# A four-stage graph network kernel: layer 0 gets a stage of its own, layers 1 and 2 share one

## The chip, the cores and the metric

The kernel runs on one core of one Trainium2 chip. The time is device microseconds of that core for the whole program, from start to end of one execution. The unchanged kernel was timed three times: 5719.75, 5727.59 and 5731.36 us, median 5727.59.

The engines are named as in the profile: PE multiplies matrices (PEld is its weight load), DVE works element by element and reduces, ACT computes activation functions and copies, SP issues DMA transfers. POOL does next to nothing here. PE's results land in PSUM, and DVE or ACT carry them on to SBUF.

## What is computed

The input is 64 independent graphs ("items") of 256 nodes with 128 features each, and a 0/1 adjacency matrix per item of 256 x 256 with about one entry in eight set. Four graph layers follow each other. After each one, the layer's input is added and the sum is normalised over the features.

```python
x = _layernorm(x + L0(x, adj))   # max over neighbours j of relu(p_i + q_j + b)
x = _layernorm(x + L1(x, adj))   # three ELU projections, adj @ in, adj.T @ out, tanh of an update
x = _layernorm(x + L2(x, adj))   # ELU twice, then two graph convolutions with D^-1/2 (A+I) D^-1/2
x = _layernorm(x + L3(x, adj))   # sum over neighbours j of gelu(layernorm(m_j + m_i + b)), update, layernorm
```

Layers 0 and 3 are the heavy ones: they compute one 128-feature message for each pair of node and neighbour, layer 0 reducing by maximum and layer 3 by a sum. Layers 1 and 2 are chains of small matrix products with ELU, tanh and layernorm between them.

## The kernel before

**Slots instead of a dense adjacency.** For each half h of the nodes j (128 of them) the kernel sorts the 256 nodes i by their number of neighbours in that half. With the nodes sorted, slot k holds the k-th neighbour of each node, and the slots' widths can shrink: 40 slots together are WIDTH columns, instead of 128 x 256. `hot` is a 0/1 matrix in fp8 that picks for each column its neighbour: PE multiplies the neighbours' features with it, in 512-column groups, in three bf16 parts each (three matmuls that add up). `lack` and `lack_t` mark columns that have no neighbour, and a few short matmuls (L681) push these out of the maximum.

**The parts of an item's work**, with the lines of the kernel before:

- *Sort and one-hots* (in `first`, L502 to L643): load `x0` and `an` (the adjacency); `nz` (L509) and its transpose `aT`; count neighbours (L528, L534); rank the nodes by ACT's Sign with an accumulator (L551); compare each rank `place` with a row of numbers to get the permutation matrices `perm` (L560); permute (L566), transpose them to `permT` (L577, L581); place the neighbours (L585), build `lack`; build `hot` with 24 comparisons and two more operations on DVE (L629, L635). The `fulls` flags go to memory by eight DMA issues (L620).
- *Layer 0* (in `first`, L644 to L712): a product of the transposed x with two weights (L647), three bf16 parts `q3`, then two times ten groups of three matmuls L665 with the `lack` matmuls, each group folded into `lanes` by DVE with a maximum (L492, called from `fold`), a maximum over the lanes `total_m` (L688), transposed (L691), back to the nodes' order (L699), the maximum of both halves `m` (L706), residual and layernorm: `x1`.
- *Layer 1* (`layer_1`, called by `second`): transpose (L207), L223, `io` (L226), ELU, L230 and `nd`, the two adjacency products L238 and L240 into `ag`, L249, `y` (L253), tanh, layernorm: `x2`.
- *Layer 2* (`layer_2`, called by `third`): L285, `hs` (L288), ELU twice, then twice: scale (L293), adjacency product L296, copy `agg` (L299), weight product L304, `hs` (L308); layernorm: `x3`.
- *Layer 3's first part* (in `third`): transpose, L797, copies `dn` and the three bf16 parts `c3` (L497 to L500), the product with `perm` L810, `dT`, and the first four of ten tiles of messages (`sums_of`): groups of three matmuls L728, added to `dT` into `pre` (L732), squared by ACT (`sq`, L736), summed over the features by PE (L743) and copied to `row` (L745); the row goes to memory, comes back in another shape, and becomes the scale 1/sqrt for each column (L74, L75), which goes to memory again.
- *Layer 3* (`last`): the scales come back, spread over the partitions (`rs_s`), `pre` is multiplied by them (L839), ACT takes Gelu (L841), DVE folds the tiles into `sums` (L492), and the remaining six tiles of `sums_of` run in between. The products L860, L870, L325, an update, two layernorms and the store end the item.

**Stages and steps.** All 64 items are unrolled. In one step, four stages work on four different items: `last` on one, `third` on the next, `second` and `first` on the two after it. Each stage is a Python generator that yields at points in its work, and `together` (L341) interleaves the stages in proportion to a number beside each of them in `STAGES` (L879), so that all four spread over the step. These numbers are `last` 34, `third` 34, `second` 14 and `first` 44. There are three steps in which the pipeline fills and three in which it drains.

**What sets the order.** The order in which the generators issue instructions is not the order on the engines: a scheduler places the instructions engine by engine, within what the buffers allow. Each engine then works through its own list strictly in order; an instruction at the head that waits holds up all behind it. PSUM has four tiles `mm` for short products and four tiles `bigp` for the 512-column groups, each kind used in turn. In the middle of the run the order repeats every two items.

ACT holds one table of functions at a time. Square, copies, Sign and Identity run with any of those used here; Gelu, Sqrt and Exp (and sometimes Tanh) each have an ACT_TABLE_LOAD in front where the function before was of another kind.

Of the kernel before, what the change touches and what calls it, by code (L numbers as in the profile page):

```python
# [9 lines left out]
F32 = mybir.dt.float32  # L10
# [33 lines left out]
def kernel(  # L44
# [17 lines left out]

    ident = consts.tile([P, P], F32, name="ident")
    make_identity(nc, ident)
    half = consts.tile([P, N], F32, name="half")
    nc.vector.memset(half, 0.5)
    eps_t = consts.tile([P, 1], F32, name="eps_t")
    nc.vector.memset(eps_t, EPS)
    minus1 = consts.tile([P, 1], F32, name="minus1")
# [284 lines left out]
    def sparse(ctx):  # L354
# [12 lines left out]
        nc.vector.tensor_copy(ident_b, ident)  # L367
        upto = cs.tile([P, P], BF16, name="upto")
        iota_k = cs.tile([P, N], F32, name="iota_k")
        down = cs.tile([1, N], BF16, name="down")  # L370
        slot1 = cs.tile([P, SLOTS], BF16, name="slot1")
        part1 = cs.tile([P, 1], F32, name="part1")
# [17 lines left out]
        with tc.tile_pool(name="cs_prep", bufs=1) as pp:  # L390
            t = pp.tile([P, P], F32, name="upto_f")
            nc.gpsimd.affine_select(
                out=t, in_=ones, compare_op=ALU.is_ge, fill=0.0, base=0, pattern=[[1, P]], channel_multiplier=-1
            )
            nc.vector.scalar_tensor_tensor(upto, ident, -FAR, t, ALU.mult, ALU.add)
            t = pp.tile([P, N], I32, name="iota_i")
            nc.gpsimd.iota(t, pattern=[[1, N]], base=0, channel_multiplier=0)
            nc.vector.tensor_copy(iota_k, t)
            t = pp.tile([P, 1], I32, name="part_i")
            nc.gpsimd.iota(t, pattern=[[0, 1]], base=0, channel_multiplier=1)  # L400
            part = pp.tile([P, 1], F32, name="part")
            nc.vector.tensor_copy(part, t)
            nc.vector.tensor_scalar(part1, part, 2.0, None, ALU.subtract)
            nc.vector.memset(part1[:3], float(SLOTS))
            nc.vector.tensor_scalar(down, iota_k[:1], -1.0, float(N - 1), ALU.mult, ALU.add)
            nc.vector.tensor_scalar(slot1, iota_k[:, :SLOTS], 1.0 - FAR, None, ALU.add)
            for h in range(H):
                for c in range(H):
                    nc.vector.tensor_scalar(
                        down_c[:, h, c:c + 1], part, -1.0, float(N - 1 - h * P), ALU.mult, ALU.add  # L410
                    )
            for t, slots in ((most, [w for s0, n, w in RECTS for _ in range(n)]), (least, SURE)):
                row = pp.tile([P, N], F32, name="slots")
                nc.vector.memset(row, 0.0)
                for w in slots:
                    if w:
                        nc.vector.tensor_scalar(row[:, :w], row[:, :w], 1.0, None, ALU.add)
                if t is most:
                    nc.vector.tensor_scalar(cover, row[:3], float(SLOTS), None, ALU.subtract)
                for hk in range(H):  # L420
                    pt = ps_mm.tile([P, 512], F32, name="mm")
                    nc.tensor.transpose(pt[:, :P], row[:, hk * P:(hk + 1) * P], ident)
                    for h in range(H):
                        nc.vector.tensor_copy(t[:, h, hk:hk + 1], pt[:, :1])
            t = pp.tile([P, 1], F32, name="gbe")
            nc.scalar.activation(t, be3, AF.Gelu)
            t3 = pp.tile([P, 3], F32, name="gbe3")
            nc.vector.tensor_copy(t3, t.broadcast_to([P, 3]))
            pt = ps_mm.tile([P, 512], F32, name="mm")
            nc.tensor.matmul(pt[:3, :P], t3, w3u[:, 1], start=True, stop=True)  # L430
            rest = pp.tile([3, P], F32, name="u_rest")
            nc.vector.tensor_copy(rest, pt[:3, :P])
            total = pp.tile([3, P], F32, name="u_total")
            nc.vector.memset(total, 0.0)
            for i in range(3):
# [12 lines left out]
            nc.vector.tensor_copy(tail, t)  # L448
            nc.vector.memset(tail[:1, g_n - 1], 1.0)
# [51 lines left out]

        def first(g, s):  # L502

            xn = sh.node_tile("x0")
            nc.sync.dma_start(xn, x[ds(g, 1)].rearrange("b (h p) d -> p (b h) d", p=P))
            an = state.tile([P, H, N], F32, name="an")
            nc.sync.dma_start(an, adj[ds(g, 1)].rearrange("b (h p) j -> p (b h) j", p=P))
            nz = pair.tile([P, H, N], BF16, name="nz")
            nc.vector.tensor_scalar(nz, an, 1.0, None, ALU.is_equal)  # L509
# [9 lines left out]
                nc.scalar.copy(aT[:, hj], pt[:, :N])  # L519
            nzT = as_bf16(aT)  # L520
            yield
            xT = sh.to_features(xn, "xT_0", 1)


            pd = psum()
# [28 lines left out]
            yield  # L554
            pos = work.tile([P, H, H], F32, name="place")
            nc.vector.tensor_scalar(pos, more, 0.5, 0.5 * (N - 1), ALU.mult, ALU.add)
            perm = state.tile([P, H, H, N], F32, name="perm", bufs=3)
            for h in range(H):
                for hi in range(H):
                    nc.vector.tensor_scalar(perm[:, h, hi], iota_k, pos[:, h, hi:hi + 1], None, ALU.is_equal)  # L560
            perm_b = as_bf16(perm)
            yield
            pz = psum()
            for h in range(H):
# [41 lines left out]
                fl[:, 5:9].rearrange("p (a b) -> p a b", a=H), fv, -1.0, least, ALU.mult, ALU.add  # L606
            )
            nc.vector.tensor_max(viol, viol, fl)
            lack_t = pair.tile([ROWS, H, g_n, g_w], BF16, name="lack_t")
            for h in range(H):  # L610
                nc.vector.tensor_mul(lack_t[:, h], tail, widen(lack[:, h, :g_w], g_n))
            s.update(an=an, aT=aT, perm=perm, permT=permT, lack=lack)

            full = pair.tile([ROWS, H, N], BF16, name="full")
            nc.vector.tensor_scalar(full, lack, 0.0, None, ALU.is_equal)
# [18 lines left out]
            for h in range(H):  # L634
# [4 lines left out]
                    ALU.is_equal,  # L639
                    saturate=False,  # L640
                )
            yield
            s["hot"] = hot  # L643

            pq = psum()
            for h in range(H):
                nc.tensor.matmul(  # L647
# [129 lines left out]

        def second(g, s):

            yield from sh.layer_1(s, s["an"], s["aT"], s["x1"])  # L780

        def third(g, s):

            dg = s["dg"]

            def deg_of(deg):
                nc.vector.tensor_scalar(deg, dg, 1.0 / N, None, ALU.mult)

            yield from sh.layer_2(s, s["aT"], deg_of)
            yield  # L790
            x3, perm = s["x3"], s["perm"]

            x3T = sh.to_features(x3, "x3T")
            yield
            pc = psum()
            for h in range(H):
                nc.tensor.matmul(  # L797
                    pc[:, h * N:(h + 1) * N], x3T[:, h * P:(h + 1) * P], w3c.rearrange("p c o -> p (c o)"),
                    start=True, stop=True,
                )  # L800
            pcv = pc.rearrange("p (h c o) -> p h c o", h=H, c=2)
            dn = work.tile([P, H, P], F32, name="dn")
            nc.scalar.copy(dn, pcv[:, :, 1])
            c3 = state.tile([P, 3, H, P], BF16, name="c3")
            split3(c3, pcv[:, :, 0])
            yield
            pd = psum()
            for h in range(H):
                for hi in range(H):
                    nc.tensor.matmul(  # L810
                        pd[:, h * N:(h + 1) * N], dn[:, hi], perm[:, h, hi], start=hi == 0, stop=hi == H - 1
                    )
            yield
            dT = state.tile([P, H, N], F32, name="dT")
            nc.scalar.activation(dT, pd.rearrange("p (h n) -> p h n", h=H), AF.Identity, bias=b3c)
            s.update(x3T=x3T, c3=c3, dT=dT)
            yield
            for i in range(AHEAD):
                yield from sums_of(s, i)
# [56 lines left out]


        U = next(u for u in (UNROLL, 8, 4, 2, 1) if B % u == 0)
        STAGES = [(last, 34), (third, 34), (second, 14), (first, 44)]  # L879

        def steps(g0):
            ss = [{} for _ in range(U)]
# [12 lines left out]
    def general(ctx):  # L895
# [10 lines left out]
        sh = Shared(work, state, ps_mm)  # L906
        psum = sh.psum
        ones3 = cs.tile([3, P], BF16, name="ones3")

        def split3(dst, src):  # L910

# [165 lines left out]

        def run():
            nc.vector.memset(ones3, 1.0)

            with tc.For_i(0, B, U) as g0:
                ss = [{} for _ in range(U)]
# [60 lines left out]
```

## Time and profile before

| | |
|---|---|
| median of three runs | 5727.59 us |
| the profiled execution | 5731.62 us |
| its span | 5729.7 us |
| busy PE / DVE / ACT | 4529.9 / 4834.4 / 4275.2 us |
| granted PE clock, mean over the run | 0.862 |
| HBM traffic over the span | 63 GB/s |
| first comparison of item 0 (`nz`) | at 35.6 us |
| first comparison of item 63 | at 5411.1 us |
| table loads on ACT | 1236, 1283 ns each |

How to read the profile: a group of the form "L560 DVE perm" is all instructions of line 560 that write the tile `perm`. Its busy time is the time in which at least one of them runs, so that busy time over count is what one adds when neighbours overlap. "PE mm L566 <- DVE perm L560: 245.5, 64, 5.1" means that PE, at L566, waited for DVE's L560 for 245.5 us in total, 64 times, the longest 5.1 us. The chain is followed back from the last instruction; each piece is what the next one waited for, or the instruction before it on the same engine. A stretch in the windows view gives for each engine the busy time within that stretch and the number of instructions.

### The profile page before, as it was taken

To read this page: it belongs to the slowest core of one execution; us is meant where nothing else is said; L and a number is where in the kernel's file an instruction comes from. 1 tells how busy PE (TensorE), PEld (TensorE's weight loads), DVE (VectorE), ACT (ScalarE), POOL (GpSimd) and SP (SyncE) were. 2 spreads that over 40 slices of the span, in tenths; PEclk is the share of its full clock that TensorE was granted. 3 is DMA by queue.
4 is the path that set the end of the run, shared out by engine and by line. 5 is a ranking of instruction groups with operands and counts; after the bars stand their busy time and mean duration, and the time that the engine had idled before them with its cause. 6 is when DMAs were issued, how large, how long until landed. Compare 5 with 4: busy or idle time off the path is not lost.

```text
span 5729.7 us, 83531 instructions
## 1 busy us (share of the span) xinstructions
PE 4529.9 (79%) x27408; PEld 2508.7 (44%) x27408; DVE 4834.4 (84%) x14654; ACT 4275.2 (75%) x6485; POOL 1.9 (0%) x10
## 2 busy tenths in 40 slices
PE   5878878878778778788788788787887887877875
PEld 2444444444444444444444444444444444444443
DVE  6788888888888888888888888888888888888876
ACT  2577777777777777777777777777777777777785
POOL 0000000000000000000000000000000000000000
PEclk8888889889889889888898898898888887888986
DMA  0122222222212221221221222122212212221222
GB/s 22 44 70 63 62 63 72 62 63 66 69 57 70 65 63 63 72 63 62 63 72 62 63 65 70 59 68 65 63 62 72 64 62 63 69 66 60 68 65 74
DMA packets 292813, 365.15 MB, mean 64 GB/s; under 512 B 151952, under 2 KB 210448, under 8 KB 292368
## 3 DMA queue, kind: packets, MB, share of 16 engines
q1 hardware_dynamic: 292368, 359.73, 20.0%
q8 instruction: 217, 3.56, 0.3%
q14 instruction: 228, 1.87, 0.1%
HBM read 345.07 MB, written 14.53 MB: 63 GB/s over the span
## 4 chain that ended last, share of the span: by engine, by line
PE 52%; DVE 29%; ACT 11%; issue 4%; DMA 3%; SPq 0%; DVEq 0%; POOL 0%; ACTq 0%
PE bigp L665 11%; PE bigp L728 8%; DVE pre L839 6%; PE mm L860 5%; DVE lanes L492 4%; PE mm L743 4%; DVE hot L629 4%; DVE pre L732 4%; DVE sums L492 3%; PE bigp L681 3%; DMA rs_s<-scale_line 2%; PE mm L870 2%; PE mm L296 2%; PE mm L699 2%; PE mm L647 2%
## 5 line engine op out<-in xcount | busy, mean ns | idle before, releaser
L665 PE MATMUL bigp<-hot,q 128*128 128x512 fp8e4 (+1 forms) x3840 | 1052.3, 371 | 66.6 <-DVE lanes L492 52.6
L728 PE MATMUL bigp<-hot,c 128*128 128x512 fp8e4 (+1 forms) x3840 | 928.8, 372 | 140.2 <-DVE pre L732 140.2
L732 DVE TENSOR_TENSOR pre<-bigp,dT 128x512 f32<-128x512 f32 (+6 forms) x1664 | 846.3, 530 | 37.8 <-PE bigp L728 33.5
L492 DVE TENSOR_TENSOR lanes<-bigp,lanes 128x512 f32<-128x512 f32 (+6 forms) x1536 | 772.7, 503 | 94.6 <-PE bigp L681 86.9
L839 DVE TENSOR_TENSOR pre<-pre,rs_s 128x1024 f32<-128x1024 f32 (+1 forms) x640 | 732.9, 1150 | 48.6 <-DMA rs_s<-scale_line 48.0
L736 ACT ACTIVATE sq<-pre 128x1024 f32<-128x1024 f32 (+1 forms) x640 | 638.5, 998 | 169.9 <-DVE pre L732 163.9
L841 ACT ACT_TABLE_LOAD x535 | 686.4, 1283 | 9.5
L492 DVE TENSOR_TENSOR sums<-pre,sums 128x1024 f32<-128x1024 f32 (+6 forms) x1024 | 628.8, 614 | 41.2 <-ACT pre L841 40.7
L745 ACT ACTIVATE row<-mm,eps_t 128x256 f32<-128x256 f32 (+1 forms) x640 | 289.6, 453 | 476.9 <-PE mm L743 476.7
L841 ACT ACTIVATE pre<-pre,be,g 128x1024 f32<-128x1024 f32 (+1 forms) x512 | 594.2, 1172 | 57.8 <-DVE pre L839 53.0
L743 PE MATMUL mm<-sq,ones 128*32 128x256 f32 (+1 forms) x5120 | 482.9, 440 | 135.2 <-ACT sq L736 135.2
L74 ACT ACT_TABLE_LOAD x445 | 570.9, 1283 | 7.5
L728 PEld LDWEIGHTS <-c 128*128 128x128 bf16 x3840 | 331.2, 98 | 550.5 <-issue 136.1
L665 PEld LDWEIGHTS <-q 128*128 128x128 bf16 x3840 | 310.8, 97 | 392.6 <-issue 112.0
L296 PE MATMUL mm<-aT,hs 128*128 128x256 f32 x512 | 232.3, 600 | 316.1 <-DVE hs L293 214.8
L629 DVE TENSOR_SCALAR hot<-rank 128x512 fp8e4<-128x512 bf16 (+5 forms) x1536 | 440.5, 348 | 0.0
L681 PEld LDWEIGHTS <-pick 42*128 42x128 bf16 x2944 | 155.8, 95 | 481.5 <-issue 474.2
L296 PEld LDWEIGHTS mm<-aT,hs 128*128 128x128 f32 x512 | 135.6, 293 | 425.8 <-issue 316.1
L860 PE MATMUL mm<-w3u,sums 128*128 128x128 f32 x2048 | 296.7, 289 | 18.4 <-DVE sums L492 16.1
L194 ACT ACT_TABLE_LOAD x221 | 283.5, 1283 | 3.9
L681 PE MATMUL bigp<-lack,pick 42*128 42x36 bf16 (+16 forms) x2944 | 285.7, 187 | 0.0
L860 PEld LDWEIGHTS mm<-w3u,sums 128*128 128x128 f32 x2048 | 254.5, 195 | 37.3 <-issue 17.6
(226 smaller groups left out, 7132.6 us busy)
## 6 DMA issues: line engine op xcount, KB each, us to landing
rs_s<-scale_line SPq DMA_DIRECT2D x512, 512.0 KB
rs_s<-scale_line SPq DMA_DIRECT2D x128, 352.0 KB
an<-in_adj SPq DMA_DIRECT2D x64, 256.0 KB
x<-in_x SPq DMA_DIRECT2D x64, 128.0 KB
line<-row SPq DMA_DIRECT2D x512, 4.0 KB
out<-o SPq DMA_DIRECT2D x64, 128.0 KB
fu<-fulls SPq DMA_DIRECT2D x192, 4.0 KB
vr<-line SPq DMA_DIRECT2D x192, 8.0 KB
```

Source lines behind the costliest of these rows:

```text
L74: nc.scalar.activation(t, t, AF.Sqrt)
L492: nc.vector.tensor_tensor(lanes[:, :k, :w], src[:, i:i + k], lanes[:, :k, :w], op)
L629: nc.vector.tensor_scalar(hot[:, :, at:at + w], rank[:, :, :w], s0 + i + 1.0 - FAR, None, ALU.is_equal, saturate=False)
L665: nc.tensor.matmul(pt[:, :tl], q3[:, i, h], hot[:, h, t0:t0 + tl], start=i == 0, stop=False)
L681: nc.tensor.matmul(o_, l_, r_, start=False, stop=i == len(todo) - 1)
L728: nc.tensor.matmul(pt[:, :bl], c3[:, k, h], hot[:, h, t0 + b:t0 + b + bl], start=k == 0, stop=k == 2)
L732: nc.vector.tensor_add(block(pre[:, b:], n, w, at), block(pt, n, w, at), widen(dT[:, h, :w], n))
L736: nc.scalar.activation(sq[:, :tl], pre[:, :tl], AF.Square)
L743: nc.tensor.matmul(pr[q * Q:(q + 1) * Q, :tl // 4], ones[:, :Q], v4[:, :, q], start=True, stop=True)
L839: nc.vector.tensor_mul(pre[:, :tl], pre[:, :tl], rs[:, :tl])
L841: nc.scalar.activation(msg[:, :tl], pre[:, :tl], AF.Gelu, bias=be3, scale=g3)
L860: nc.tensor.matmul(pt[:, cols], lanes[:, k, cols], w3u[:, 1], start=k == 0, stop=False)
```

## The change

Layer 0 moves out of `first` into a function `layer_0`, which `second` now runs; layer 1 moves from `second` to `third`, ahead of layer 2. So the four stages are: sort and one-hots; layer 0; layers 1 and 2 with layer 3's first four tiles; layer 3. The numbers in `STAGES` become 34, 48, 28 and 17.

Tiles that now live for more steps get more buffers or another pool: `x0` and `an` have three, and `lack_t` moves to the pool `state`, where it has two. `perm` becomes bf16, written by comparing a bf16 row of numbers; layer 3, which multiplies with it in f32, makes an f32 copy `perm_f` on ACT for each item. The tile `half` is made only in the general path, which does not run with these inputs.

```diff
-            xn = sh.node_tile("x0")
+            xn = state.tile([P, H, P], F32, name="x0", bufs=3)
...
-            an = state.tile([P, H, N], F32, name="an")
+            an = state.tile([P, H, N], F32, name="an", bufs=3)
...
-            xT = sh.to_features(xn, "xT_0", 1)
...
-            perm = state.tile([P, H, H, N], F32, name="perm", bufs=3)
+            perm = state.tile([P, H, H, N], BF16, name="perm", bufs=3)
             for h in range(H):
                 for hi in range(H):
-                    nc.vector.tensor_scalar(perm[:, h, hi], iota_k, pos[:, h, hi:hi + 1], None, ALU.is_equal)
-            perm_b = as_bf16(perm)
+                    nc.vector.tensor_scalar(perm[:, h, hi], iota_b, pos[:, h, hi:hi + 1], None, ALU.is_equal)
+            perm_b = perm
...
-            lack_t = pair.tile([ROWS, H, g_n, g_w], BF16, name="lack_t")
+            lack_t = state.tile([ROWS, H, g_n, g_w], BF16, name="lack_t")
...
-            yield
             s["hot"] = hot

+        def layer_0(s):
+
+            xn, hot, lack, lack_t, permT = (s[n] for n in ("xn", "hot", "lack", "lack_t", "permT"))
+            xT = sh.to_features(xn, "xT_0", 1)
+            yield
             pq = psum()
...
         def second(g, s):

+            yield from layer_0(s)
+
+        def third(g, s):
+
             yield from sh.layer_1(s, s["an"], s["aT"], s["x1"])
-
-        def third(g, s):
-
+            yield
             dg = s["dg"]
...
-            x3, perm = s["x3"], s["perm"]
+            x3 = s["x3"]
+            perm = work.tile([P, H, H, N], F32, name="perm_f")
+            nc.scalar.copy(perm, s["perm"])
...
-        STAGES = [(last, 34), (third, 34), (second, 14), (first, 44)]
+        STAGES = [(last, 34), (third, 48), (second, 28), (first, 17)]
```

More of the change, by code (lines that the diff above doesn't have):

```diff
@@ L64 @@
     make_identity(nc, ident)
-    half = consts.tile([P, N], F32, name="half")
-    nc.vector.memset(half, 0.5)
     eps_t = consts.tile([P, 1], F32, name="eps_t")
@@ L369, in sparse @@
         iota_k = cs.tile([P, N], F32, name="iota_k")
+        iota_b = cs.tile([P, N], BF16, name="iota_b")
         down = cs.tile([1, N], BF16, name="down")
@@ L398, in sparse @@
             nc.vector.tensor_copy(iota_k, t)
+            nc.vector.tensor_copy(iota_b, t)
             t = pp.tile([P, 1], I32, name="part_i")
@@ L608, in first @@
             nc.vector.tensor_max(viol, viol, fl)
-            lack_t = pair.tile([ROWS, H, g_n, g_w], BF16, name="lack_t")
+            lack_t = state.tile([ROWS, H, g_n, g_w], BF16, name="lack_t")
             for h in range(H):
                 nc.vector.tensor_mul(lack_t[:, h], tail, widen(lack[:, h, :g_w], g_n))
-            s.update(an=an, aT=aT, perm=perm, permT=permT, lack=lack)
+            s.update(xn=xn, an=an, aT=aT, perm=perm, permT=permT, lack=lack, lack_t=lack_t)
             full = pair.tile([ROWS, H, N], BF16, name="full")
@@ L641, in first @@
                 )
+            s["hot"] = hot
+        def layer_0(s):
+            xn, hot, lack, lack_t, permT = (s[n] for n in ("xn", "hot", "lack", "lack_t", "permT"))
+            xT = sh.to_features(xn, "xT_0", 1)
             yield
-            s["hot"] = hot
             pq = psum()
@@ L908, in general @@
         ones3 = cs.tile([3, P], BF16, name="ones3")
+        half = cs.tile([P, N], F32, name="half")
         def split3(dst, src):
@@ L1079, in run @@
             nc.vector.memset(ones3, 1.0)
+            nc.vector.memset(half, 0.5)
             with tc.For_i(0, B, U) as g0:
```

## The prediction

> **What bounds the kernel now.** I read the page first, then two items in the middle of the run by windows, then the chain over the same stretch, then the waits.
>
> ```profile
> span 5729.7 us, 83531 instructions
> PE 4529.9 (79%) x27408; PEld 2508.7 (44%) x27408; DVE 4834.4 (84%) x14654; ACT 4275.2 (75%) x6485; POOL 1.9 (0%) x10
> ```
>
> No engine is full. The profiled execution took 5731.6 us (span plus 1.9), 4.0 above the median of 5727.6. The work of `nz` (L509), one per item, starts at 262.2 us for item 4 and at 5411.1 for item 63: 87.3 us an item. Cut one item at the ends of three PE lines of the chain (L699 at 2905.5, L304 at 2943.6, L810 at 2962.5, L699 again at 2992.1):
>
> ```profile
> 2905.50:2943.60 38.10, 22.12 (x121) 12.36 (x118) 30.49 (x97) 33.66 (x54) 0.00 (x0) 0.78 0.15 46
> 2943.60:2962.50 18.90, 18.44 (x110) 9.07 (x110) 16.89 (x50) 13.18 (x18) 0.00 (x0) 1.00 0.31 103
> 2962.50:2992.10 29.60, 28.16 (x205) 17.03 (x206) 27.54 (x85) 19.62 (x30) 0.00 (x0) 1.00 0.22 67
> ```
>
> Columns: stretch, us, then busy PE, PEld, DVE, ACT, POOL, clock. In the last two stretches PE is busy 46.6 of 48.5 us: PE bounds them. In the first PE is busy 22 of 38, while DVE has 30.5 and ACT 33.7: here the sort, layer 1's start and layer 2 stand together on PE with hardly a long group of matmuls between them. The busiest engines add to 33.7 + 18.4 + 28.2 = 80.3 of 86.6 us; 6.3 us an item are lost in handing over, 4.4 of them in the first stretch. The chain and the waits name the places:
>
> ```profile
> 2924.15 1.16 PE mm L566 x4
> ...
> 2939.31 2.05 PE mm L296 x4
> ...
> 2943.06 0.56 PE mm L304 x4
> ...
> 2960.52 1.99 PE mm L810 x8
> ```
> ```profile
> PE mm L566 <- DVE perm L560: 245.5, 64, 5.1
> PE mm L296 <- DVE hs L293: 214.8, 67, 8.7
> DVE io L226 <- PE mm L223: 179.7, 64, 3.1
> ACT sq L736 <- DVE pre L732: 163.9, 128, 2.7
> ```
>
> Per item: PE 3.8 us for the permutation and 3.4 for layer 2's `hs`, DVE 2.8 for layer 1's first product.
>
> **The change part by part.**
>
> *Conversions.* `perm` in bf16: 4 x 64 comparisons of 284 ns each (72.7 us over 256). Two rows bound the new price: nothing saved, or the third that `full` (42x512, a comparison in bf16, 278 ns) saves against `nz` (f32, 421): 0.4 us an item. I take 0: by the table below these stand where PE is the longer engine. Added is `perm_f`, one ACT copy of 1024 elements an item: 1.05 us by `sq` (128x1024, 1052 ns) to 1.24 by the Gelu row; 67 to 79 us of ACT in all. In the changed program's order it is issued after `dT` (L822), before the first `sq` of the next tiles, which waits 2.6 us an item for `pre` today (163.9/64). I take 0; without that cover it is 1.05 us an item, 67 us, and behind it on ACT would stand `sq` and `row`, for which L743 on PE waits. `lack_t` and the third buffers of `x0` and `an` move no instruction; DVE waited for `an` once, 3.6 us, so 0 there. `iota_b` is one cast (0.3 us) and `half` leaves the prologue (0.27): 0.
>
> *ACT's tables.* Counted in the two orders, table loads fall from 1236 (as in the trace) to 1183: Gelu -71, Sqrt -64, Exp +63, Tanh +19. 53 x 1283 ns = 68 us, which the copy eats: ACT's total stays. The Exp loads, one more an item, stand in layers 1 and 2, on the chain of the new third stage. Bounds: 0, where ACT loads while it waits for DVE (it waits 85.8 us for `rs`, its load already done), and 1.28 us an item, where the chain waits for the load. I take 0, since DVE has 1.6 to 3.5 us of other work between handing over and each Exp's result.
>
> ```profile
> 2804.13 1.28 ACT L74 ACT_TABLE_LOAD   x1
> 2805.42 0.20 ACT L74 ACTIVATE rs<-rs 128x2 f32<-128x2 f32 x1
> ```
>
> The activation follows the load within 0.01 us. The Trainium skill ("ScalarE: Activation LUTs", What ACT_TABLE_LOAD costs) adds a 1380 ns drain to each load; by that the 53 loads would be an estimated 141 us and ACT would gain 74. This trace shows no drain, so the sum goes by 68.
>
> *Moved stages.* Every instruction and DMA stays: PE 27408, and 8 `fulls` issues, 10 `line`, 10 `rs_s` and the loads an item on SP's queue. Only order moves. Moved past others on SP are the `fulls` issues, now among the `line` issues of other tiles; DVE waits 48.0 us in all for `rs_s` (0.75 an item), and I keep that, bounded by 0 and twice. The order is a scheduler's, not the program's, so I read it from the built program and work out its cost as for before: per engine, between two points that the third stage's chain ties together, the rows' busy time over count, less 60 ns for each DVE and 43 ns for each ACT instruction (neighbours overlap; this brings an item to the measured 75 and 67 us). Mean of the three patterns that alternate in the new order, us:
>
> | from - to | PE | DVE | ACT |
> |---|---|---|---|
> | layer 1's `io` - layer 2's first `hs` (L226 - L288 before) | 31.4 | 25.2 | 26 |
> | `hs` - layer 3's `c` ready (L288 - L500) | 20.1 | 32.4 | 27 |
> | `c` - next `io` | 17.0 | 17.4 | 14 |
>
> The third row's longer engine, pattern by pattern, is 18.0, so 31.4 + 32.4 + 18.0 = 81.8 us against 80.3 before. The losses come on top. Gone: L534 to L566 had 2.3 us of other PE work between them and waited 3.8, so the chain needs 6.1; now 16.7 stand between. L304 to the second L296: 0.8 before, 7.6 now. `total_m`'s transposes to L699: 0, now 2.0. New: L304 to L797 (layer 2's end, layernorm, transposes) had 17.9 us of PE work, now 2.6; L207, L797, L810 and L728 follow each other directly, where each hand-over is an ACT copy of 0.37 us; L240 to L249 14.5, now 1.8 (`ag` 0.58, covered). Behind the waiting L207 the whole of PE's queue stands, layer 0's and layer 3's groups too. DVE has its own work meanwhile (6.6 us between L308 and `x3`, then 5.7 to `c`), which is why the second row counts as DVE's. `x1` to `io` keeps its wait: 2.9 us of DVE work plus 2.95 of wait today; 1.1 of work after, and fewer PE rows ahead of L223, so 2.2 taken, between 1.9 and 4.7. L2's two loops: L293 to L308 has 3.2 us of DVE work on the mean and takes 4.1 to 6 (5.9 seen at 3028.4 to 3034.3, with L647 ahead of L304): 1.0 taken each. `y` (L330) keeps its 1.05; layernorms and ELU 0.5, PSUM tiles 0.5. Sum 2.2 + 2.0 + 1.05 + 1.0 = 6.25, as much as is lost today. Low: the two bounded kinds of stretch as today's PE-bound ones, 3.5%, 2.8 us. High: all DVE-bound time (50.4 us) at the first stretch's 4.4/33.7, 6.6, plus 1.6 for the PE-bound: 8.2.
>
> 81.8 + 6.3 = 88.1 against 87.3: +0.8 us for some 60 full items, +50.
>
> *Ends.* Fill: item 0 runs 48 us through sort and layer 0 (35.6 to 83.8) before item 1's turn; now 19. The third step becomes layers 1, 2 and four tiles, against 72 us now (135.9 to 207.7): for item 0, layer 2 to the fourth tile took 63 (135.9 to 199), and layer 1 lies between 20 (its rows one after the other) and the 44 from 83.8 to 127.8, where sort and layer 0 of item 1 ran in between; I take 22, so 85. The second step, layer 0 beside a sort, is about 33 us by its DVE rows against 52 (83.8 to 135.9). Full steps start some 35 us sooner: 29 + 19 - 13. Drain: layer 0 of item 63 and layer 1 of 62 and 63 now lie in it; the 78 and 65 us steps (5531 to 5609 to 5674) grow by about 10 and 20. Net 0, between -35 and +30.
>
> 5731.6 + 50 = 5781.6; in the scale of the median, 5778.
>
> **Rivals.**
> 1. *The filler works (faster).* The 6.3 us of `hot` building (L629, L635), in one block after the sort today, are spread through the step in the new order and cover DVE's hops; PE's 3.8 and most of 3.4 are saved. Loss 2.8: 84.6 us, -2.7 x 60 = -160: 5568. It decides once the loss falls below 5.5. Against: the waits of DVE, not of PE, must shrink, and `io`'s does not. The Trainium skill ("Perfetto Trace Analysis", Optimization Strategy) says that interleaving regimes with different busiest engines may help; this speaks for it and against my forecast, and today's first stretch is such a regime.
> 2. *Serial third stage (much slower).* Layers 1, 2 and the first tiles become one chain in one step, and PE starves at L207-L728 without getting it back. Loss 9.5: 91.3, +4.0 x 60 = +240: 5968.
> 3. *Nothing moves.* Loss 5.5: 5728.
>
> **How the numbers follow.** Forecast (5740 to 5870) 0.39; rival 1 0.36; rival 2 0.19; rival 3 0.06. 0.2% (11 us) is what can be told from no change. Faster 0.36, same 0.06, slower 0.58. The range reaches to rival 1's middle and near rival 2's: 5575 to 5945, leaving a tenth at each end.
>
> **What would show it.** Right: the wait of L566 under 30 us in all; L207 for `x` over 250 us (107.8 now); `io`'s still over 100; DVE under 84.5%; 1183 table loads. Wrong: DVE at 87% or more (rival 1), or PE's waits for `x` and `c` over 500 us (rival 2). ACT waited for at `perm_f` by L810 would refute its cover.

## The result and the profile after

The changed kernel takes 5794.36 us (median of four runs, 5793.36 to 5806.16); the kernel before, in the runs beside them, 5729.48 (5719.75 to 5735.55). The ratio is 1.012, with a 95% interval of 1.010 to 1.0139: slower by 65 us, against a forecast of 50. The profiled execution has a span of 5792.0 us, 62.3 longer than before.

The head of the page and its line of the chain (part 4, shares of the span):

```profile
span 5792.0 us, 83294 instructions
PE 4510.3 (78%) x27408; PEld 2445.6 (42%) x27408; DVE 4812.7 (83%) x14654; ACT 4278.2 (74%) x6496; POOL 2.0 (0%) x10
PE 50%; ACT 25%; DVE 16%; DMA 4%; issue 4%; SPq 1%; ACTq 0%; DVEq 0%; POOL 0%; POOLq 0%
```

The same line of the chain before the change:

```profile
PE 52%; DVE 29%; ACT 11%; issue 4%; DMA 3%; SPq 0%; DVEq 0%; POOL 0%; ACTq 0%
```

PE, DVE and ACT each have as much work as before, to within 22 us; what grew is idle time. On the chain ACT's share went from 11 to 25%, DVE's fell from 29 to 16%.

Some of PE's groups before and then after the change, each in order of cost. Behind the bar stand the busy time, the mean of one instruction, and the idle time just before the group, with what ended it:

```profile
L665 PE MATMUL bigp<-hot,q 128*128 128x512 fp8e4 (+1 forms) x3840 | 1052.3, 371 | 66.6 <-DVE lanes L492 52.6 <-DVE q L499 11.0 <-DVE pre L732 1.1
...
L743 PE MATMUL mm<-sq,ones 128*32 128x256 f32 (+1 forms) x5120 | 482.9, 440 | 135.2 <-ACT sq L736 135.2
...
L296 PE MATMUL mm<-aT,hs 128*128 128x256 f32 x512 | 232.3, 600 | 316.1 <-DVE hs L293 214.8 <-DVE vr L769 101.3
L207 PE MATMUL mm<-ident,x 128*128 128x128 f32 x512 | 148.8, 356 | 107.8 <-DVE x L180 107.8
...
L797 PE MATMUL mm<-w3c,x3T 128*128 128x256 f32 x256 | 71.8, 403 | 1.0 <-ACT x3T L209 1.0
```

```profile
L668 PE MATMUL bigp<-hot,q 128*128 128x512 fp8e4 (+1 forms) x3840 | 1077.7, 378 | 338.4 <-ACT lanes L686 138.2 <-DVE pre L735 117.5 <-DVE lanes L492 40.1
L731 PE MATMUL bigp<-hot,c 128*128 128x512 fp8e4 (+1 forms) x3840 | 948.4, 373 | 78.0 <-DVE pre L735 66.8 <-DVE lanes L492 8.1
L746 PE MATMUL mm<-sq,ones 128*32 128x256 f32 (+1 forms) x5120 | 441.8, 421 | 220.3 <-ACT sq L739 220.1
...
L294 PE MATMUL mm<-aT,hs 128*128 128x256 f32 x512 | 199.7, 529 | 15.6 <-DVE hs L291 15.6
L817 PE MATMUL mm<-perm_f,dn 128*128 128x256 f32 x512 | 194.3, 543 | 40.8 <-ACT dn L810 40.8
L205 PE MATMUL mm<-ident,x 128*128 128x128 f32 x512 | 141.0, 386 | 328.2 <-DVE x L178 328.2
...
L804 PE MATMUL mm<-w3c,x3T 128*128 128x256 f32 x256 | 131.8, 669 | 56.9 <-ACT x3T L207 56.9
...
L565 PE MATMUL mm<-perm,nz 128*128 128x256 bf16 x256 | 51.5, 277 | 7.7 <-DVE perm L559 7.6
```

This is a balance. Two waits are gone: that for the permutation (L566 before, L565 now) from 245.5 us to 7.7, and that of layer 2's adjacency product (L296 before, L294 now) from 316.1 to 15.6; together 538 us. Other waits took their place: x at L205 (L207 before) from 107.8 to 328.2, layer 0's groups (L665, now L668) from 66.6 to 338.4, the feature sums (now L746) from 135.2 to 220.3, L804 from 1.0 to 56.9: together 633 us. Other lines went either way (L731 fell by 62). PE's idle time in all rose from 1199.8 us (span less busy) to 1281.7, that is 82 us; PE is 20 us less busy; the difference is the 62 us.

The wait for x can be split by layer, since ACT's copy behind each pair of transposes names the layer. After the change 267 of the 328 us are waits for x3, the end of layer 2; before, none of the 108 us is. That is the hand-over for which the prediction saw PE's other work shrink from 17.9 to 2.6 us.

Three items in the middle of the run, cut at the same points as the forecast's table (`io`, the first `hs`, `c` ready, next `io`); columns as in the windows before:

```profile
2553.60:2580.20 26.60, 25.84 (x168) 12.94 (x168) 23.31 (x65) 23.38 (x39) 0.00 (x0) 0.96 0.30 96
2580.20:2617.20 37.00, 23.50 (x120) 12.06 (x121) 33.47 (x94) 28.41 (x36) 0.00 (x0) 0.82 0.22 69
2617.20:2641.10 23.90, 20.81 (x145) 13.30 (x148) 17.61 (x73) 13.43 (x26) 0.00 (x0) 0.93 0.14 42
2641.10:2669.80 28.70, 26.64 (x175) 12.67 (x172) 25.51 (x70) 27.39 (x42) 0.00 (x0) 1.00 0.31 92
2669.80:2706.10 36.30, 22.31 (x116) 12.04 (x115) 34.53 (x101) 29.19 (x39) 0.00 (x0) 0.76 0.20 56
2706.10:2731.60 25.50, 22.32 (x144) 13.71 (x146) 15.02 (x60) 12.03 (x24) 0.00 (x0) 0.83 0.12 37
2731.60:2762.30 30.70, 27.65 (x175) 13.07 (x171) 25.30 (x69) 28.68 (x43) 0.00 (x0) 0.98 0.27 88
2762.30:2794.70 32.40, 21.02 (x114) 11.53 (x115) 30.41 (x93) 24.03 (x34) 0.00 (x0) 0.79 0.20 62
2794.70:2819.90 25.20, 20.28 (x145) 12.55 (x147) 18.98 (x69) 14.61 (x26) 0.00 (x0) 0.97 0.08 22
```

Means of the three items, us:

| stretch | length | busiest engine | lost | forecast: busiest |
|---|---|---|---|---|
| `io` to `hs` | 28.7 | 27.3 (PE or ACT) | 1.4 | 31.4 |
| `hs` to `c` | 35.2 | 32.8 (DVE) | 2.4 | 32.4 |
| `c` to next `io` | 24.9 | 21.1 (PE) | 3.7 | 18.0 |
| an item | 88.8 | 81.2 | 7.5 | 81.8, and 6.3 lost |

From `nz` to `nz` an item takes 88.81 us on the mean of items 8 to 59, 1.57 more than before on the same measure (87.24).

### The profile page after: what moved, and what is told of

Same layout as the page of the kernel before. It is cut to its first block, busy times and chain, and to the rows that moved or that the text cites. A ratio compares the mean times of both kernels' runs of the same rounds, so it can differ in the third digit from the quotient of the medians.

```text
span 5792.0 us, 83294 instructions
## 1 busy us (share of the span) xinstructions
PE 4510.3 (78%) x27408; PEld 2445.6 (42%) x27408; DVE 4812.7 (83%) x14654; ACT 4278.2 (74%) x6496; POOL 2.0 (0%) x10
## 4 chain that ended last, share of the span: by engine, by line
PE 50%; ACT 25%; DVE 16%; DMA 4%; issue 4%; SPq 1%; ACTq 0%; DVEq 0%; POOL 0%; POOLq 0%
PE bigp L668 10%; PE bigp L731 6%; PE mm L746 5%; ACT pre L848 5%; ACT sq L739 3%; ACT L72 3%; ACT L848 3%; PE mm L817 3%; PE mm L867 3%; PE mm L294 3%; DMA rs_s<-scale_line 3%; PE bigp L684 2%; PE mm L877 2%; PE mm L221 2%; DVE pre L846 2%
## 5 line engine op out<-in xcount | busy, mean ns | idle before, releaser
L668 PE MATMUL bigp<-hot,q 128*128 128x512 fp8e4 (+1 forms) x3840 | 1077.7, 378 | 338.4 <-ACT lanes L686 138.2
L731 PE MATMUL bigp<-hot,c 128*128 128x512 fp8e4 (+1 forms) x3840 | 948.4, 373 | 78.0 <-DVE pre L735 66.8
L735 DVE TENSOR_TENSOR pre<-bigp,dT 128x512 f32<-128x512 f32 (+6 forms) x1664 | 851.1, 530 | 48.5 <-PE bigp L731 42.7
L492 DVE TENSOR_TENSOR sums<-pre,sums 128x1024 f32<-128x1024 f32 (+6 forms) x1024 | 628.8, 614 | 29.7 <-ACT pre L848 28.7
L746 PE MATMUL mm<-sq,ones 128*32 128x256 f32 (+1 forms) x5120 | 441.8, 421 | 220.3 <-ACT sq L739 220.1
L668 PEld LDWEIGHTS <-q 128*128 128x128 bf16 x3840 | 301.2, 98 | 584.2 <-DVE pre L735 136.0
L731 PEld LDWEIGHTS <-c 128*128 128x128 bf16 x3840 | 344.7, 100 | 478.1 <-issue 129.6
L628 DVE TENSOR_SCALAR hot<-rank 128x512 fp8e4<-128x512 bf16 (+5 forms) x1536 | 483.8, 348 | 0.0
L205 PE MATMUL mm<-ident,x 128*128 128x128 f32 x512 | 141.0, 386 | 328.2 <-DVE x L178 328.2
L867 PE MATMUL mm<-w3u,sums 128*128 128x128 f32 x2048 | 295.2, 288 | 50.1 <-DVE sums L492 50.1
L746 PEld LDWEIGHTS mm<-sq,ones 128*32 128x32 f32 x5120 | 106.5, 114 | 470.5 <-ACT sq L739 316.3
L867 PEld LDWEIGHTS mm<-w3u,sums 128*128 128x128 f32 x2048 | 253.5, 194 | 103.4 <-DVE sums L492 54.7
```

The costliest lines, as they stand in the source:

```text
L492: nc.vector.tensor_tensor(lanes[:, :k, :w], src[:, i:i + k], lanes[:, :k, :w], op)
L628: nc.vector.tensor_scalar(hot[:, :, at:at + w], rank[:, :, :w], s0 + i + 1.0 - FAR, None, ALU.is_equal, saturate=False)
L668: nc.tensor.matmul(pt[:, :tl], q3[:, i, h], hot[:, h, t0:t0 + tl], start=i == 0, stop=False)
L731: nc.tensor.matmul(pt[:, :bl], c3[:, k, h], hot[:, h, t0 + b:t0 + b + bl], start=k == 0, stop=k == 2)
L735: nc.vector.tensor_add(block(pre[:, b:], n, w, at), block(pt, n, w, at), widen(dT[:, h, :w], n))
L746: nc.tensor.matmul(pr[q * Q:(q + 1) * Q, :tl // 4], ones[:, :Q], v4[:, :, q], start=True, stop=True)
```

## The experiments

Each run is given with its ratio to the kernel before, taken beside it. Differences between two changed kernels are of medians; by the ratios they come out up to 10 us otherwise.

The theory: a step is a little slower because layers 1, 2 and the first tiles now form one chain in one stage, and PE, which works strictly in order, stands before L205 until DVE has finished x. The rivals: the conversions cost it, above all ACT's copy; or PSUM's tiles do; or the order alone does, whatever is moved.

### The conversions in the old stages

```diff
-            perm = state.tile([P, H, H, N], F32, name="perm", bufs=3)
+            perm = state.tile([P, H, H, N], BF16, name="perm", bufs=3)
...
-            x3, perm = s["x3"], s["perm"]
+            x3 = s["x3"]
+            perm = work.tile([P, H, H, N], F32, name="perm_f")
+            nc.scalar.copy(perm, s["perm"])
```

> The kernel before with its old four stages, and only the conversions of the change: perm in bf16 and its f32 copy perm_f on ACT. Theory of the prediction (conversions are hidden, the move of the stages makes the whole difference): 5729 us within 0.4% (5706 to 5752). Rival (the ACT copy of about 1.05 us an item lies on the path): half or more of the 65 us that the change cost, 5760 to 5795.

Measured: 5740.39 us against 5722.11 for the kernel before, a ratio of 1.0032 (1.0018 to 1.0046). The conversions cost 18 us (10 to 26 by the interval), 0.3 us an item: small, and inside the 0.4% that the theory allowed, but not 0. DVE gains 18 us in the comparisons (from 347 to 278 ns each, 256 of them). ACT gets 66 us of copies, and its busy time rises from 4275.2 to 4331.7. Nobody waits for `perm_f`: PE's L814 waits for `dn`. PE's wait for the permutation stays, so it is not the conversions that took it away:

```profile
PE mm L568 <- DVE perm L562: 240.7, 64, 5.4
```

### The copy made twice, in the changed kernel

```diff
             nc.scalar.copy(perm, s["perm"])
+            nc.scalar.copy(perm, s["perm"])
```

> The changed kernel with the ACT copy perm_f made twice for each item. Theory (hidden behind the wait for pre): 5794 us within 0.4% (5771 to 5817). Rival (ACT's time counts in full, about 1.05 us for 64 items): 5850 to 5865 us.

Measured: 5828.99 us, 1.0196 (1.0174 to 1.0217) of the kernel before, so 35 us above the changed kernel (44 by the ratios): 0.5 to 0.7 us an item of the 1.03 that a copy takes. The second copy isn't hidden, but not wholly on the path either. It is no clean price: the order shifted as well, and 1209 table loads ran in place of 1183 (26 x 1.283 = 33 us of ACT's time).

### Layer 1 back in the second stage, behind layer 0

```diff
         def second(g, s):
             yield from layer_0(s)
+            yield
+            yield from sh.layer_1(s, s["an"], s["aT"], s["x1"])
         def third(g, s):
-            yield from sh.layer_1(s, s["an"], s["aT"], s["x1"])
-            yield
...
-        STAGES = [(last, 34), (third, 48), (second, 28), (first, 17)]
+        STAGES = [(last, 34), (third, 34), (second, 42), (first, 17)]
```

> The changed kernel with layer 1 moved back from the third stage to the second, behind layer 0; the numbers beside the stages are 34, 34, 42, 17. Theory (the loss comes from one serial chain of layers 1, 2 and the first tiles in the third stage, seen as PE waiting for x): PE's wait for x at the transposes falls from 328 us to under 200, and the time to 5560 to 5720 us, below the kernel before. Rival (the loss comes from the new order as a whole, from PSUM tiles and the end of the step, not from the third stage's length): 5760 to 5830 us.

Measured: 5587.84 us (5587.15 to 5589.52), 0.9772 (0.9751 to 0.9792) of the kernel before: faster than both kernels, and 3.5% below the changed one. All other parts of the change are in it. An item takes 85.33 us. PE's groups:

```profile
L668 PE MATMUL bigp<-hot,q 128*128 128x512 fp8e4 (+1 forms) x3840 | 1120.9, 392 | 205.6 <-DVE lanes L492 179.7 <-ACT q L497 17.7 <-DVE q L499 4.7
...
L205 PE MATMUL mm<-ident,x 128*128 128x128 f32 x512 | 150.1, 375 | 55.6 <-DVE x L178 55.5
...
L650 PE MATMUL mm<-w0qp,xT 128*128 128x256 f32 x256 | 129.9, 661 | 266.1 <-ACT xT L207 266.1
```

The wait for x fell from 328.2 to 55.6 us, and L668's from 338.4 to 205.6; none of the wait that is left at L205 is for x3. A new wait stands at layer 0's start (L650, 266.1), where ACT is late with the transposed x0. PE's idle time in all is 1067 us, 215 below the changed kernel's.

### The third stage's share of the interleaving: 60 and 40 in place of 48

```diff
-        STAGES = [(last, 34), (third, 48), (second, 28), (first, 17)]
+        STAGES = [(last, 34), (third, 60), (second, 28), (first, 17)]
```

> The changed kernel with 60 instead of 48 beside the third stage, so that its chain runs ahead and ends at about four fifths of the step, where the other stages have work left behind it. Theory (the chain has too little time for each hand-over at 48, and less at 60): 5800 to 5900 us. Rival (the chain's end at the end of the step, with nothing left to cover it, is what costs): 5650 to 5770 us.

Measured: 5878.14 us, 1.0269 (1.0243 to 1.0295), within what the theory expected. The wait for x more than doubled:

```profile
PE mm L205 <- DVE x L178: 710.1, 128, 7.3
```

But the time rose by 84 us only, not by the 382 of this wait: L668's wait fell to 206.3 us and L746's to 46.4, and PE's idle time in all rose by 23 us (to 1305). The rest of the 84 is PE's busy time (4570.7 us, 60 more) at a granted clock of 0.857 against 0.881. So the wait for x (315 us of it for x3, the rest for layers 1 and 2) shows where PE stands, and not what the standing costs.

```diff
-        STAGES = [(last, 34), (third, 48), (second, 28), (first, 17)]
+        STAGES = [(last, 34), (third, 40), (second, 28), (first, 17)]
```

> The changed kernel with 40 instead of 48 beside the third stage, so that it runs behind the others and ends alone. Theory (the hand-overs get more time while the others run, but the end stands alone): 5790 to 5900 us. Rival (the order is arbitrary at the level of one per cent): anywhere from 5720 to 5860, and e9 likewise, so that 1.2% could not be laid to the chain's length alone.

Measured with 40: 6392.28 us, 1.1159 (1.1123 to 1.1195), outside what either side expected. PE's idle time grew by 363 us against the changed kernel and its busy time by 255, at a granted clock of 0.814. The largest wait stands at the last stage's products L867. The profile puts it down to DVE's `dinv` (L272), a value of the third stage, but L867 reads no `dinv`. First the row of the waits, then one of them in order of time:

```profile
PE mm L867 <- DVE dinv L272: 763.1, 60, 13.1
```
```profile
3187.02 0.17 DVE L492 TENSOR_TENSOR sums<-part_add,sums 128x12 f32<-128x12 f32 x1
3187.11 0.15 DVE L272 TENSOR_TENSOR dinv<-dinv,pos 128x2 f32<-128x2 f32 x1
...
3187.34 0.55 PE L867 MATMUL mm<-w3u,sums 128*128 128x128 f32 x1 [12.69 <-DVE dinv L272]
```

What L867 multiplies are the `sums`, whose last fold ends 0.15 us before it starts, here and at the other long waits; `dinv` merely runs next on DVE. So PE stands for 12.7 us before the products of the stage that is finishing, until that stage's last fold is done, and everything behind them in PE's queue waits as well: in the stretch shown x3 was finished at 3182.54, and its transposes (L205) ran at 3195.25. No instruction was added: a number beside a stage moved the time by 10%.

### No layer 1

```diff
-            yield from sh.layer_1(s, s["an"], s["aT"], s["x1"])
-            yield
+            s["x2"] = s["x1"]
...
-        STAGES = [(last, 34), (third, 48), (second, 28), (first, 17)]
+        STAGES = [(last, 34), (third, 34), (second, 28), (first, 17)]
```

> The changed kernel with layer 1 left out (layer 2 takes layer 0's output, so the result differs); numbers 34, 34, 28, 17. It prices layer 1 by where it stands. Its engine work, by rows of the profile before, is about 5 us PE, 6 us DVE and 4 us ACT an item. Theory (in the second stage layer 1 costs about its DVE work, in the third it costs its latency on top): 5150 to 5350 us, so that layer 1 costs 240 to 440 us in the second stage and 440 to 640 in the third. Rival (layer 1's work is hidden in the second stage, and what the third pays is only queueing at its own hand-overs): 5500 to 5588 us.

Measured: 5136.48 us, 0.8971 (0.8948 to 0.8994), with layer 1 left out. The wait at L205 is 6.9 us. Against this floor layer 1 costs 451 us where it stands in the second stage (5587.84) and 658 where it stands in the third (5794.36): 7.1 and 10.3 us an item. The time lies 14 us below what the theory expected, and both prices 11 to 18 us above; they hold all that goes with layer 1, ACT's table loads too (953 ran here).

### Five tiles for the long groups, three for the short products

```diff
-        ps_mm = ctx.enter_context(tc.tile_pool(name="ps_mm", bufs=4, space=bass.MemoryType.PSUM))
-        ps_big = ctx.enter_context(tc.tile_pool(name="ps_big", bufs=4, space=bass.MemoryType.PSUM))
+        ps_mm = ctx.enter_context(tc.tile_pool(name="ps_mm", bufs=3, space=bass.MemoryType.PSUM))
+        ps_big = ctx.enter_context(tc.tile_pool(name="ps_big", bufs=5, space=bass.MemoryType.PSUM))
```

> The changed kernel with five PSUM tiles for the 512-column groups and three for the short products, in place of four and four. Theory (PE's waits for x and the short hops of the third stage set the loss): not faster, 5790 to 5900 us, since fewer tiles for the short products hold the sort and layer 1 back. Rival (PE's new waits at layer 0's groups for PSUM tiles, 256 us in all, set it): 5680 to 5760 us.

> Layer 1 in the second stage and PSUM divided into five `bigp` tiles and three for the rest. In the third stage of the changed kernel this division was worth 34 us; matmuls that wait for a `bigp` tile hold some 180 us behind the lanes' evictions with layer 1 in the second stage, too. If those waits are on the path: 5520 to 5570. Against it: 1272 table loads are written, 120 more than without it, which at the 0.3 to 1.3 us between the runs here would take 36 to 150 us: 5600 to 5740.

Measured in the changed kernel: 5759.93 us, 1.0065 (1.004 to 1.0091), 34 us faster than with four and four and at the upper end of what the PSUM rival expected. With layer 1 in the second stage: 5653.31, 0.9871 (0.9854 to 0.9887), 65 us slower than with four and four. The sign turns over. In the first case 127 table loads fewer ran (1056 against 1183), in the second 120 more (1272 against 1152), so the fifth tile's own effect can't be read from either run.

### The f32 permutation, and two buffers for `an`

The changed stages with an f32 permutation need more SBUF than there is with three buffers of `an`, so this run has two:

```diff
-            an = state.tile([P, H, N], F32, name="an", bufs=3)
+            an = state.tile([P, H, N], F32, name="an", bufs=2)
...
-            perm = state.tile([P, H, H, N], BF16, name="perm", bufs=3)
+            perm = state.tile([P, H, H, N], F32, name="perm", bufs=3)
...
-            x3 = s["x3"]
-            perm = work.tile([P, H, H, N], F32, name="perm_f")
-            nc.scalar.copy(perm, s["perm"])
+            x3, perm = s["x3"], s["perm"]
```

> The kernel with layer 1 behind layer 0 in the second stage (5588 us), and the conversions undone: perm in f32 as before, no copy perm_f; an has two buffers, which is enough where layer 1 stands in the second stage. Theory (about half of the ACT copy is on the path, 18 us by the conversions alone and 35 us by the second copy): 5555 to 5575 us. Rival (in this order the copy is hidden): 5588 us within 0.2%, 5577 to 5599.

Measured, with layer 1 in the second stage: 5885.38 us, 1.0275 (1.0247 to 1.0304), 298 us slower than with the bf16 permutation, and far from both expectations. It differs in two things, so the next run keeps the bf16 permutation and its copy and changes only the buffers:

```diff
-            an = state.tile([P, H, N], F32, name="an", bufs=3)
+            an = state.tile([P, H, N], F32, name="an", bufs=2)
```

> Layer 1 in the second stage, the bf16 permutation and its copy kept, but the pool `an` with two buffers instead of three. If the f32 permutation cost the 297 us between the two runs with layer 1 in the second stage (5885 against 5588), this run is near the faster of them: 5560 to 5640. If it is the third buffer of `an`, through the order that it lets the work take (the written program loads an activation table 1274 times here, as often as in the 5885 run, and 1152 times in the 5588 run), it is near the slower: 5840 to 5900. A time in between shares the loss between the two.

Measured: 5890.72 us, 1.0291 (1.0274 to 1.0308). So the whole difference comes with the third buffer of `an` and the order that is built with it; the permutation's type is worth nothing that shows here. The timeline with two buffers (start, duration in us, engine, line):

```profile
2677.64 0.81 PE L238 MATMUL mm<-an,io 128*128 128x256 f32 x3
...
2678.48 0.38 SPq L507 DMA_DIRECT2D an<-in_adj  x1
...
2681.24 0.42 DVE L509 TENSOR_SCALAR nz<-an 128x512 bf16<-128x512 f32 x1
```

and with three:

```profile
2544.49 0.41 DVE L509 TENSOR_SCALAR nz<-an 128x512 bf16<-128x512 f32 x1
...
2545.97 1.03 PE L238 MATMUL mm<-an,io 128*128 128x256 f32 x4
...
2547.03 0.39 SPq L507 DMA_DIRECT2D an<-in_adj  x1
```

In both, the load is issued 0.03 us after layer 1's last product with the old `an`: it waits for the buffer. With two buffers it is the load for the very sort that stands next, and `nz` follows 2.8 us behind L238, bound to it. With three it is the load for one item later; `nz` starts 2.5 us before L238 ends, its load issued 83 us earlier (median over the items; 2.8 us with two buffers). An item takes 90.16 us in place of 85.33, and 1274 table loads run in place of 1152. The tie is shown; how 5.3 us of delay at `nz` become 4.8 us an item was not followed through the engines. In the kernel before, which has two buffers of `an` too, the load is issued 13 us ahead of `nz` (median), so it isn't bound in this way; it was not run with three.

### Is the fast version a lucky order?

```diff
-        STAGES = [(last, 34), (third, 34), (second, 42), (first, 17)]
+        STAGES = [(last, 34), (third, 38), (second, 42), (first, 17)]
```

> Layer 1 in the second stage, the third stage's share of the fourth's tiles changed from the 42 of that run to 38. If the gain belongs to the place of layer 1, and the exact order matters little, the time is within 1% of 5588: 5535 to 5645. If the 5588 run was a lucky order, this one falls back toward the changed kernel: 5700 or more. 1159 table loads are written against 1152.

Measured: 5594.55 us, 0.9766 (0.975 to 0.9783). The next run makes the copy on POOL:

```diff
-            nc.scalar.copy(perm, s["perm"])
+            nc.gpsimd.tensor_copy(perm, s["perm"])
```

> Layer 1 in the second stage, and the f32 copy of the permutation made on POOL, which is idle (2.0 us busy), instead of ACT. The copy took ACT 1.03 us an item; a second copy cost 35 us in the changed kernel. If half of it is on the path as there: 5550 to 5575. If POOL needs much longer for the copy and the combination's matmul waits for it, or POOL and DVE disturb each other: 5590 to 5660.

Measured: 5592.38 us, 0.9764 (0.9748 to 0.978). Both ratios agree with that of the run they start from (0.9772). So the place holds its gain under one changed share. Taking the copy off ACT gained nothing: neither the 13 to 38 us that were expected with half a copy an item on the path, nor was there a clear loss. Either the copy is hidden there, or what it gave up was lost again on DVE, whose busy time grew by 27.6 us beside POOL's copies; this run alone does not tell. The two runs with two buffers, one with the copy and one without, differ by nothing that shows either. The copy's price is a matter of what stands around it: 18 us for both conversions in the old stages, nothing that shows here.

Over all runs with three buffers of `an`: layer 1 in the second stage gave 5588, 5592, 5595 and 5653 us, layer 1 in the third 5760, 5794, 5829 (copy twice), 5878 and 6392. The two groups don't overlap. With two buffers layer 1 in the second stage gave 5885 and 5891, so the place alone isn't the whole answer.

## Why the prediction was right, and which of its steps were not

**The sign, the size and the case were right**: 5794 measured, 5778 forecast, within the forecast's own range (5740 to 5870). All five signs that were named appeared: the permutation's wait 7.7 us (under 30), x at L205 328 (over 250), `io` still waiting, DVE at 83%, and 1183 table loads, as counted in the order:

```profile
DVE io L224 <- PE mm L221: 183.4, 64, 3.6
L848 ACT ACT_TABLE_LOAD x464 | 595.3, 1283 | 8.0
L72 ACT ACT_TABLE_LOAD x381 | 488.8, 1283 | 9.4 <-DMA vr<-line 2.8
L192 ACT ACT_TABLE_LOAD x254 | 325.9, 1283 | 4.5
L196 ACT ACT_TABLE_LOAD x62 | 79.5, 1283 | 1.1
```

(464 + 381 + 254 + 62, and 22 more in smaller groups.) Neither sign of a wrong forecast came: DVE is below 87%, and PE's waits on the way from x to `dn` (L205, L804, L817) add to 426 us, below 500.

**The sum hit its mark through two errors that largely cancel, and that is luck.** "88.1 against 87.3: +0.8 us for some 60 full items, +50" was +1.57, worth 97 us over 62 items. "Net 0, between -35 and +30" for the ends was -35: the first output is finished at 236.5 us in place of 292.2 (-56, forecast -35), and the drain is about 20 longer (forecast +30). 97 - 35 = 62, against 50 + 0.

**The busiest engines' sum was right to 0.6 us** (81.8 forecast, 81.2 in the windows), but not stretch by stretch: work of PE's stands 4 us less in the first and 3 more in the third.

**The loss was mis-sized**: 6.3 forecast, 7.5 measured, inside its bound of 8.2. The term that was furthest off is "PSUM tiles 0.5". Layer 0's groups (L668) wait for a `bigp` tile, 138.2 us for ACT's `lanes` and 117.5 for DVE's `pre`: 4.0 us an item of PE's idle time, at a line that the prediction did not name. Not all of it is on the path, and the runs with five tiles don't give its price, so it isn't shown that this term makes up the 1.2 us. A second term is "`y` (L330) keeps its 1.05", which became 2.4 (156.6 us over 64). The wait for `hs` at L296 was read as 3.4 us an item and is 4.9 (316.1 us over 64): L296 reads no `vr`, so the 101.3 us that the profile puts down to `vr` belong to it. The lower bound, 3.5% as in "today's PE-bound ones", comes out at 3.9% by its own rows (those two stretches lost 1.9 of 48.5 us), which moves the bound to 3.2 us and changes nothing here.

**"I take 0" for the conversions was wrong in the old stages, by 18 us.** The step said that the copy is covered by `sq`'s wait for `pre`. The sign to refute it, that L810 (now L817) waits for `perm_f`, was badly chosen: no such wait appeared (L817 waits for `dn`), and the time was paid all the same. For the changed kernel there is only the second copy's 35 us, with a changed order. With layer 1 in the second stage no price shows.

**The mechanism of rival 2, "PE starves at L207-L728", was present in small**: 328 us at L205. The runs with 60 and with layer 1 moved back show its sign and place, and that most of it is the wait for x3. Its cost in time is not the wait's length, as the 60 run shows: 382 us of wait more, 84 us of time.

**Rival 1 (the filler works) did not come about**: the two waits of PE that it meant to save were saved, 538 us of them, but came back at other lines, and the loss is 7.5 us an item, not below the 5.5 at which it decides. A time near its 5568 came with layer 1 in the second stage (5588), where an item takes 85.33 us; the loss there was not measured stretch by stretch.

The changed stages kept at two buffers of `an` were not run. What stays open: how much of the 65 us belongs to layer 1's place and how much to the particular order that came out. Single numbers moved the time by 84 us and 598 us.

## What to carry to other kernels

Waits in a full pipeline aren't prices: 538 us of PE's waits went away here and 633 came back elsewhere, so a forecast needs the engines' sum per stretch and the ends, and not the waits that disappear. Where the profile names what ended a wait, see in the code whether the waiting instruction reads it: `dinv` above was only the neighbour of what was waited for. Where a scheduler sets the order, try a moved stage with more than one share: here one arrangement ranged from 5794 to 6392 us. When a stage moves, ask for each loaded tile which late reader frees its buffer: one more buffer of `an` was worth some 300 us, more than the whole change.

## What the runs showed of the hardware

**The granted clock is lower where PE idles, and matmuls there take longer.** In the windows above PE's mean granted clock is 0.96 to 1.00 in the first stretches (busy 25.84 of 26.6 us in the first of them) and 0.76 to 0.82 in the second (busy 22 of 36). The third stretches don't fit as neatly: 0.93, 0.83 and 0.97, with PE busy for 80 to 88%. The trace's clock records hold two values only, full and half, and the windows show means of these. The same instruction on operands of the same shape (min/median/max in ns), in the kernel before, in the changed one, and with layer 1 in the second stage:

```profile
L810 PE MATMUL mm<-perm,dn x512: 379/379/796, 176.7 to 5640.2; 128*128 128x256 f32 x171
```
```profile
L817 PE MATMUL mm<-perm_f,dn x512: 379/631/796, 133.9 to 5708.1; 128*128 128x256 f32 x171
```
```profile
L817 PE MATMUL mm<-perm_f,dn x512: 379/379/797, 138.4 to 5491.2; 128*128 128x256 f32 x171
```

After the change 315 of L817's 512 matmuls start while the clock is at half, with a median of 634 ns, and the others take 379; before, 5 of 512 do. L817's busy time rose by 67 us (127.2 to 194.3), and ACT's `dT` behind it waits 121.3 us. Layer 2's adjacency product won back 33 (232.3 to 199.7). Over the whole run PE's busy time stayed within 20 us: the low clock fell on other instructions. The Trainium skill ("TensorE: Matmul & The Clock Gate", Part 1) says that the throttled clock is the default and that sustained matmuls release it, which agrees in kind.

**A copy on POOL held up one of DVE's operations.** With the copy on POOL (78.3 us busy), DVE's busy time grew by 27.6 us. Nearly all of it is one comparison an item that builds `hot`, with a single source in SBUF. First this size of comparison with the copy on ACT (layer 1 in the second stage), then with the copy on POOL:

```profile
L628 DVE TENSOR_SCALAR hot<-rank 128x284 fp8e4<-128x284 bf16 x128 | 36.4, 286 | 0.0
```
```profile
L628 DVE TENSOR_SCALAR hot<-rank 128x284 fp8e4<-128x284 bf16 x128 | 60.4, 473 | 0.0
```

60 of these 128 comparisons run beside POOL's copy and take 675 ns on the mean; the other 68 take 295. One of the 60, with the copy:

```profile
2611.81 1.24 POOL L798 CAST perm_f<-perm 128x1024 f32<-128x1024 bf16 x1 [84.14 <-PE mm L817]
...
2612.53 0.67 DVE L628 TENSOR_SCALAR hot<-rank 128x284 fp8e4<-128x284 bf16 x1
```

In all 60 the comparison ends 0.16 to 0.17 us behind the copy, whether it took 0.67 or 0.84 us. DVE's four largest groups moved by 2 to 3 us each (instructions of different groups overlap, so these don't add up). The Trainium skill ("SBUF — State Buffer", SBUF: two separate sides) describes a port pair that DVE and GpSimd take from each other for a whole instruction. The rows agree in kind: the comparison ends at a fixed time behind the copy, as if held until then.
